# Four source blocks of attention products as one run on TensorE, the last pair of blocks first

## The chip, the cores and the metric

The kernel runs on one core of a Trainium2 chip. A core has several engines that work side by side: TensorE for matrix products (in the profile PE for the products and PEld for the loads of the stationary operand), VectorE (DVE), ScalarE (ACT), GpSimd (POOL) and a queue for transfers (SP). Each engine takes its own list of instructions in a fixed order, and semaphores hold an instruction back until what it reads has been written, or until the buffer that it writes has been read out.

The metric is the time on the device of one execution, in microseconds (us). Before the change it was 3025.95 us, the median of 3 runs (3025.94 to 3026.56). The profile is of one further execution, with a span of 3023.3 us.

## What is computed

Four graph-attention layers run one after the other over 16 graphs of 1024 nodes with 256 features. Each layer normalises the features, cuts them at zero, attends over the graph's neighbours and adds the result to its input. Layer 3, which the change touches, has four heads of 64 features. Cut to what matters:

```
h     = einsum('bnd,hde->bhne', relu(layernorm(x)), W)
weight[i, j] = leaky_relu(e_src[i] + e_dst[j])  where there is an edge
attention    = softmax(weight, over the sources j)
dst   = einsum('bhij,bhje->bhie', attention, h) + bias
out   = layernorm over a head's 64 features (relu(dst) + h) * gamma + beta
x     = x + out
```

The softmax is not normalised ahead of the product. For each head the kernel forms sums of values, each source's features times its unnormalised weight, and beside them totals, the sums of the weights alone, and divides the first by the second at the end.

## The kernel before

**Two streams.** `batch(b)` is a Python generator that writes out the work of one graph and yields estimates of its time. `stream(0)` takes the even graphs and `stream(1)` the odd ones, and the loop at the end of `short_path` (lines 624 to 634) always advances the stream whose estimated clock is behind; the second starts 111 us later (`LAG`). While one stream is in layer 3, the other is in layers 0 to 2 of its graph. The order in which the code is written out is a priority, not the order in which it runs. The framework's scheduler builds each engine's list: of the instructions that are ready in its own model of the run, it takes the one that was written out first. Two means bend this order: `tc.keep_in_program_order(x)` puts x behind the instruction of the same engine that was written out just before it, and `tc.high_priority()`, a context, lets what is written inside it go ahead of ready work outside it.

**Layers 0 to 2** (`attend`, lines 393 to 444). `weigh` (lines 306 to 322) first lets TensorE spread a row of factors over all partitions of the PSUM tile `row` (8 transposes, line 314). There is a single `row` buffer for both streams. VectorE then makes 8 weight tiles of 128 x 1024 out of it, one for each block of 128 source nodes (line 318). Products with line 409 follow, 128 x 128 stationary by 257 moving columns: for the first two blocks of target nodes as each weight tile appears, for the other six afterwards. `project` (lines 267 to 302) makes the values for the next layer: transposes on line 290, products on line 297.

**Layer 3** (lines 478 to 615). Here the values are stationary and the weights move, so that 512 target nodes stream through at once. A head's 64 features and its totals do not fill the array. So `in_tiles` gives each product 32 columns of the array, one of four quadrants (`QUAD` is 32), and four products with different quadrants can run together. All of these matmuls stand on line 517. For a pair of source blocks, `add_values` makes 8 matmuls (two blocks, two halves of the targets, two parts of the features) into the PSUM tile `acc`, and `add_totals` makes 4 (two blocks, two halves) into the PSUM tile `total`. The trace shows each float32 matmul as two records, so that a pair's values are 16 records and its totals 8.

For head 0 the values of each pair follow as soon as VectorE has made the pair's two weight tiles; the totals follow after the row for head 1 is begun, four blocks to a chunk. For heads 1 to 3 a chunk of four blocks has totals and values together: 24 matmuls, 48 records. `pinned`, emptied at the start of every chunk, is the list of the chunk's matmuls so far: from the second on, each is kept behind the one before. That settles the order inside a chunk. It does not keep other ready work of TensorE from coming in between.

The weight tiles of a stream live in 8 buffers (`edges`, `bufs=NI`). So the next head's tiles can only be written when the chunks that read the old ones are through. When a head is finished, ScalarE copies `acc` and `total` out (line 579), TensorE turns them (lines 586 and 594), and VectorE, ScalarE and GpSimd divide, add the bias and normalise (lines 483 to 502).

Of the kernel before, what the change touches and what calls it, by code (L numbers as in the profile page):

```python
# [19 lines left out]

# [2 lines left out]

# [34 lines left out]
def short_path(ctx: ExitStack, tc: tile.TileContext, ins: dict, out: bass.AP, bad: bass.AP):  # L60

    nc = tc.nc
# [3 lines left out]
    NI = N // P  # L66
# [6 lines left out]
    QUAD = P // 4  # L73
# [190 lines left out]
    def accumulator(b: int) -> bass.AP:  # L264
        return psum.tile([P, HALF], F32, name=f"acc{b % 2}")
# [58 lines left out]
    def start(behind, b: int):  # L324

        for t in behind:
            if row_taken == [b]:
                return
            yield t

    def inverse(inv: bass.AP, total: bass.AP):

        nc.vector.tensor_scalar_max(inv, total, TINY)  # L333
        nc.vector.reciprocal(inv, inv)  # L334
# [14 lines left out]
    def batch(b: int):  # L349
# [23 lines left out]
        last = {}  # L373
# [109 lines left out]
        def center(h: int):  # L483

            yh = y[:, :, h, :]
            head = ts(h, E)
            nc.gpsimd.tensor_add(yh, yh, bias[:, head].unsqueeze(1).to_broadcast(shape))  # L487
            nc.vector.scalar_tensor_tensor(yh, yh, 0.0, h3[:, :, head], op0=ALU.max, op1=ALU.add)
            mean = small.tile([P, NI], F32, name="mean")
            nc.vector.tensor_reduce(mean, yh, AX.X, ALU.add)  # L490
            nc.vector.tensor_scalar_mul(mean, mean, 1.0 / E)
            nc.vector.tensor_sub(yh, yh, mean.unsqueeze(2).to_broadcast(shape))
            square = wide.tile(shape, F32, name="wide", bufs=1)
            nc.scalar.activation(square, yh, AF.Square)
            var = small.tile([P, NI], F32, name="var")
            nc.vector.tensor_reduce(var, square, AX.X, ALU.add)  # L496
            return yh, head, inverse_root(var, NI, E, L3_EPS)

        def rescale(yh: bass.AP, head, rstd: bass.AP):
            nc.vector.tensor_mul(yh, yh, rstd.unsqueeze(2).to_broadcast(shape))  # L500
            nc.gpsimd.tensor_mul(yh, yh, gamma[:, head].unsqueeze(1).to_broadcast(shape))
            nc.gpsimd.tensor_add(yh, yh, xb[:, :, head])
# [3 lines left out]
        def weigh3(h: int):  # L506
            if h == H:
                return iter(())
            return weigh(
                b, lambda i: ex[:, i, 2 * H + h : 2 * H + h + 1],  # L510
                lambda j: ex[:, j, H + h : H + h + 1], ALU.max, weights,
            )

        def in_tiles(parts, accT: bass.AP, first: bool, last: bool):

            for n, (values, moving) in enumerate(parts):
                made = nc.tensor.matmul(  # L517
                    accT[ts(n, QUAD), :], values, moving, start=first, stop=last
                )

                if pinned:
                    tc.keep_in_program_order(made)
                pinned.append(made)

        def halves_of(h: int, j: int):
            return [weights[h * NI + j][:, ts(g, HALF)] for g in range(NH)]

        def add_values(h: int, j: int):

            for n in (j + 1, j):  # L530
                parts = [
                    (V3[:, n, h, ts(e, QUAD)], moving)
                    for moving in halves_of(h, n)
                    for e in range(2)
                ]
                in_tiles(parts, acc, n == 1, n == NI - 2)

        def add_totals(h: int, j: int):

            parts = [  # L540
                (V3[:, j + n, h, E:].to_broadcast([P, QUAD]), halves_of(h, j + n)[g])
                for g, n in ((0, 1), (0, 0), (1, 1), (1, 0))
            ]
            in_tiles(parts, total, j == 0, j == NI - 2)

        behind = weigh3(0)
        yield from start(behind, b)
        for h in range(H):


            acc = accumulator(b)
            total = accumulator(b)
            if h == 0:
                for j in range(0, NI, 2):
                    next(behind)
                    next(behind)
                    pinned = []
                    add_values(h, j)
                    yield 1.8
                for _ in behind:  # L560
                    pass
            behind = weigh3(h + 1)
            yield from start(behind, b)
            step = 4
            for first in range(0, NI, step):
                pinned = []
                for j in range(first, first + step, 2):
                    add_totals(h, j)
                    if h > 0:
                        add_values(h, j)  # L570
                for _ in range(step):
                    next(behind, None)
                yield 1.8 if h == 0 else 5.4
            for _ in behind:
                pass
            copies = []
            for accT in (acc, total) if h == 0 else (total, acc):
                copies.append(wide.tile([P, HALF], F32, name="sums"))
                nc.scalar.copy(copies[-1], accT)  # L579
                next(testing)  # L580
                next(coming, None)
            sums, totals = copies if h == 0 else copies[::-1]
            yield 0.5
            turned = psum.tile([P, NG, P], F32, name="misc")
            for i in range(NG):
                nc.tensor.transpose(turned[:, i, :], totals[:, ts(i, P)], ident)  # L586
            inv = small.tile([P, NH, NG], F32, name="inv8")
            nc.vector.tensor_reduce(
                inv, turned[:, :, ::QUAD].rearrange("p i (g n) -> p g i n", n=2), AX.X, ALU.add
            )  # L590
            inverse(inv, inv)
            turned = psum.tile([P, NG, NH, E], F32, name="misc")
            for i in range(NG):
                nc.tensor.transpose(  # L594
                    turned[:, i].rearrange("p g e -> p (g e)"), sums[:, ts(i, P)], ident
                )
            nc.vector.tensor_mul(
                y[:, :, h, :].rearrange("p (g i) e -> p g i e", g=NH),
                turned.rearrange("p i g e -> p g i e"),
                inv.unsqueeze(3).to_broadcast([P, NH, NG, E]),  # L600
            )
            yield 0.5
            if h > 0:
                rescale(*normed.pop())
            normed.append(center(h))
            yield 1.0
# [11 lines left out]
    def stream(first: int):  # L618
        for _ in loading[first]:
            yield 2.0  # L620
        for b in range(first, B, 2):
            yield from batch(b)
# [389 lines left out]
```

## Time and profile before

| what | value |
|---|---|
| time, median of 3 | 3025.95 us |
| span of the profiled run | 3023.3 us |
| granted TensorE clock, mean over the span | 0.993 of full |
| VectorE busy | 2112.7 us, 70% |
| ScalarE busy | 1092.1 us, 36% |
| GpSimd busy | 964.5 us, 32% |
| idle time of VectorE before line 318, ended by line 517 | 51.0 us in 30 waits |

The work repeats. In the chain of work that ended last, the run of 32 matmuls of line 409 that starts at 1165.17 us comes again at 1349.19 us, 184.02 us later, and so on through the run. In each such period one stream does its layer 3 while the other does part of its layers 0 to 2; two periods make a graph of one stream. One period is therefore enough to read, and I use the one from 1065 to 1249 us.

A timeline line gives the start, the time from the first start to the last end of a group of equal instructions, the engine, the line of code, the operation, the tiles and the number of instructions; in brackets the idle time of the engine before it, and what ended it. Matmuls overlap, so that the time a group takes up is read from its start to the start of the next line, not from the second column. In the page's groups "busy" is the union of the times of all instructions of a group and "mean ns" the duration of one of them.

### The profile page before, as it was taken

How to read it: one execution, taken by the hardware profiler on the slowest of the kernel's cores; microseconds unless marked ns; L12 is line 12 of the kernel's file. 1: busy time of each engine (PE TensorE's matmuls, PEld its weight loads, DVE VectorE, ACT ScalarE, POOL GpSimd, SP SyncE). 2: the span in 40 equal slices, each digit the busy share in tenths (PEclk: the TensorE clock that was granted, in tenths of full speed). 3: DMA queues.
4: the chain of work that ended last, by engine and by line, in shares of the span. 5: the costliest groups of instructions: out<-in, count | busy, mean ns of one | idle time of the engine just before them, and what ended most of it. 6: DMA issues, size and time to landing. Idle time of an engine off the chain costs nothing.

```text
span 3023.3 us, 44588 instructions
## 1 busy us (share of the span) xinstructions
PE 2905.2 (96%) x16774; PEld 1960.1 (65%) x16774; DVE 2112.7 (70%) x4467; ACT 1092.1 (36%) x3009; POOL 964.5 (32%) x1455
## 2 busy tenths in 40 slices
PE   7999999999999999999999999999999999999985
PEld 5775857658576675756758566585766857667551
DVE  5657687676866758677576875758667686675756
ACT  2333424243343433424334243433434334243331
POOL 2124324142232423324233242432324234242333
PEclk9999999999999999999999999999999999999997
DMA  7204023030321403122040220302204031110101
GB/s 122 37 8 63 29 29 56 8 49 29 36 49 14 71 2 49 36 28 57 5 50 31 29 56 8 50 29 32 53 11 56 19 50 36 15 29 5 19 21 30
DMA packets 120495, 106.11 MB, mean 35 GB/s; under 512 B 73680, under 2 KB 91216, under 8 KB 120272
## 3 DMA queue, kind: packets, MB, share of 16 engines
q0 software_dynamic: 40448, 67.12, 15.2%
q1 hardware_dynamic: 79824, 36.05, 5.9%
q8 instruction: 135, 2.21, 0.3%
q14 instruction: 88, 0.72, 0.1%
HBM read 153.49 MB, written 33.55 MB: 62 GB/s over the span
## 4 chain that ended last, share of the span: by engine, by line
PE 78%; DVE 12%; POOL 4%; ACT 4%; issue 2%; DMA 1%; SPq 0%; ACTq 0%; POOLq 0%; DVEq 0%
PE acc L409 39%; PE acc L517 21%; PE acc L297 11%; DVE weights L318 6%; PE misc L290 3%; PE row L314 2%; POOL rstd L261 2%; POOL y L487 1%; DVE y L500 1%; DVE V L365 1%; DVE var L496 1%; PE misc L594 1%; ACT adj_i L143 1%; ACT square L281 1%; PE misc L586 1%
## 5 line engine op out<-in xcount | busy, mean ns | idle before, releaser
L409 PE MATMUL acc<-V,weights 128*128 128x257 f32 x6144 | 1452.5, 386 | 24.6 <-ACT above L343 12.8
L409 PEld LDWEIGHTS acc<-V,weights 128*128 128x128 f32 x6144 | 1135.1, 190 | 338.3 <-DVE weights L318 92.7
L517 PE MATMUL acc<-weights,V 128*32 128x512 f32 x6144 | 756.4, 598 | 3.6 <-DVE weights L318 3.6
L318 DVE SCALAR_TENSOR_TENSOR weights<-row,ex,mask 128x1024 f32<-128x1024 f32 x512 | 631.2, 1276 | 91.0 <-PE acc L517 51.0
L297 PE MATMUL acc<-W,hT 128*128 128x259 f32 (+1 forms) x2048 | 522.1, 391 | 39.8 <-ACT hT L292 28.2
L297 PEld LDWEIGHTS acc<-W,hT 128*128 128x128 f32 x2048 | 376.5, 190 | 165.2 <-issue 49.5
L318 DVE SCALAR_TENSOR_TENSOR weights<-row,V,mask 128x1024 f32<-128x1024 f32 x384 | 475.4, 1276 | 7.7 <-PE row L314 7.7
L517 PEld LDWEIGHTS acc<-weights,V 128*32 128x32 f32 x6144 | 174.1, 109 | 379.6 <-issue 370.6
L341 ACT ACTIVATE below<-acc,inv 128x256 f32<-128x256 f32 x256 | 121.3, 474 | 681.0 <-DVE inv L334 404.1
L261 POOL TENSOR_TENSOR rstd<-rstd,minus_half 128x2 f32<-128x2 f32 (+1 forms) x320 | 307.7, 962 | 20.3
L281 ACT ACTIVATE square<-x_b,minus_mean 128x256 bf16<-128x256 f32 x512 | 259.2, 506 | 136.4 <-DVE minus_mean L271 131.7
L333 DVE TENSOR_SCALAR inv<-acc 128x1 f32<-128x1 f32 x256 | 39.7, 155 | 302.5 <-PE acc L409 299.0
L389 POOL TENSOR_TENSOR x_b<-x_b,beta 128x256 f32<-128x256 f32 x128 | 93.6, 731 | 491.1 <-ACT square L281 491.1
L579 ACT COPY sums<-acc 128x512 f32<-128x512 f32 x128 | 75.0, 586 | 413.9 <-PE acc L517 413.9
L260 POOL TENSOR_SCALAR rstd<-squared 128x2 f32<-128x2 f32 x256 | 59.5, 233 | 504.4 <-ACT square L281 503.6
L361 ACT ACTIVATE V<-acc,rstd 128x3 f32<-128x3 f32 x384 | 98.5, 262 | 315.2 <-PE acc L297 312.9
L292 ACT ACTIVATE hT<-misc 128x512 f32<-128x512 f32 x256 | 150.5, 594 | 155.4 <-PE misc L290 155.0
L365 DVE TENSOR_SCALAR V<-acc,rstd,V 128x256 f32<-128x256 f32 x256 | 133.1, 539 | 78.0 <-ACT V L361 77.2
L274 DVE TENSOR_SCALAR centered<-x_b,minus_mean 128x256 f32<-128x256 f32 x512 | 180.4, 383 | 4.3
L138 POOL DMA_DIRECT2D adj_i<-in_adj_dram x128 | 75.6, 590 | 331.0 <-ACT adj_i L143 262.2
L344 DVE SCALAR_TENSOR_TENSOR x_b<-below,x_b 128x256 f32<-128x256 f32 x256 | 117.7, 460 | 87.6 <-ACT below L341 87.4
L290 PE MATMUL misc<-ident,centered 128*128 128x128 f32 x1024 | 159.7, 278 | 15.7 <-DVE centered L274 13.8
(76 smaller groups left out, 2224.8 us busy)
## 6 DMA issues: line engine op xcount, KB each, us to landing
adj_i<-in_adj_dram POOLq DMA_DIRECT2D x128, 256.0 KB, 3.9
x_b<-in_x_dram SPq DMA_DIRECT2D x16, 1024.0 KB, 6.4
narrow<-in_adj_dram POOLq DMA_DIRECT2D x64, 256.0 KB, 9.5
out_dram<-y POOLq DMA_DIRECT2D x32, 512.0 KB, 7.5
mask<-narrow SPq DMA_TRANSPOSE x64, 4.3
W<-in_L_gnn_W_dram SPq DMA_DIRECT2D x3, 256.0 KB, 6.9
weights<-in_L_gnn_a_dram SPq DMA_DIRECT2D x3, 256.0 KB, 9.0
W<-in_L_gnn_W_dram SPq DMA_DIRECT2D x2, 128.0 KB, 7.9
```

Source lines behind the costliest of these rows:

```text
L261: nc.gpsimd.tensor_tensor(r, r, minus_half.to_broadcast([P, n]), op=ALU.pow)
L274: nc.vector.tensor_scalar(centered[:, n, :], xb[:, 2 * pair + n, :], minus_mean[:, n : n + 1], 0.0, op0=ALU.add, op1=ALU.max,)
L281: nc.scalar.activation(square, xb[:, 2 * pair + n, :], AF.Square, bias=minus_mean[:, n : n + 1], accum_out=squared[:, n : n + 1],)
L290: nc.tensor.transpose(turned[:, k, ts(n, P)], centered[:, n, ts(k, P)], ident)
L292: nc.scalar.mul(hT, turned, ROOT_D)
L297: nc.tensor.matmul(projected, hT[:, k, ts(n, P)], W[l][:, k, :], start=(k == 0), stop=(k == NK - 1),)
L318: nc.vector.scalar_tensor_tensor(w, r, c(j), masks[b][:, j // 2, :, j % 2], op0=op, op1=ALU.mult)
L341: nc.scalar.activation(below, acc[:, :D], AF.Exp, scale=inv)
L344: nc.vector.scalar_tensor_tensor(xi, below, 1.0, xi, op0=ALU.min, op1=ALU.add)
L365: nc.vector.tensor_scalar(V[:, i, :D], projected[:, :D], rstd, V[:, i, D : D + 1], op0=ALU.mult, op1=ALU.mult,)
L409: nc.tensor.matmul(accs[i], weights[j][:, ts(i, P)], V[:, j, : D + 1], start=(j == 0), stop=(j == NI - 1),)
L517: made = nc.tensor.matmul(accT[ts(n, QUAD), :], values, moving, start=first, stop=last)
```

## The change

The change lets TensorE run the layer-3 products of four source blocks as one run that nothing interrupts. Three edits work together:

- every matmul of a chunk but the first is written out under `tc.high_priority()`, so that once a chunk has begun, its rest goes ahead of other ready work;
- the two pairs of a chunk are taken in turned order (`first + 2`, then `first`), so that the chunk's first matmul waits for its last-made weight tile, and the others find theirs made; the flags that open and close an accumulation move with the order (blocks 3 and 4 in place of 1 and 6, pairs 2 and 4 in place of 0 and 6);
- head 0's values, in chunks of two blocks until now, come in chunks of four. The estimate yielded for a chunk doubles with it, from 1.8 to 3.6.

The operations and their number stay the same; only their order moves.

```diff
-                made = nc.tensor.matmul(
-                    accT[ts(n, QUAD), :], values, moving, start=first, stop=last
-                )
-
+
+                with tc.high_priority() if pinned else nullcontext():
+                    made = nc.tensor.matmul(
+                        accT[ts(n, QUAD), :], values, moving, start=first, stop=last
+                    )
                 if pinned:
                     tc.keep_in_program_order(made)
                 pinned.append(made)
...
-                in_tiles(parts, acc, n == 1, n == NI - 2)
+                in_tiles(parts, acc, n == 3, n == NI - 4)
...
-            in_tiles(parts, total, j == 0, j == NI - 2)
+            in_tiles(parts, total, j == 2, j == NI - 4)
...
             if h == 0:
-                for j in range(0, NI, 2):
-                    next(behind)
-                    next(behind)
+                for first in range(0, NI, 4):
+                    for _ in range(4):
+                        next(behind)
                     pinned = []
-                    add_values(h, j)
-                    yield 1.8
+                    for j in (first + 2, first):
+                        add_values(h, j)
+                    yield 3.6
                 for _ in behind:
                     pass
             behind = weigh3(h + 1)
             yield from start(behind, b)
-            step = 4
-            for first in range(0, NI, step):
+
+            for first in range(0, NI, 4):
                 pinned = []
-                for j in range(first, first + step, 2):
+                for j in (first + 2, first):
                     add_totals(h, j)
                     if h > 0:
                         add_values(h, j)
-                for _ in range(step):
+                for _ in range(4):
                     next(behind, None)
                 yield 1.8 if h == 0 else 5.4
```

More of the change, by code (lines that the diff above doesn't have):

```diff
@@ L23 @@
-from contextlib import ExitStack
+from contextlib import ExitStack, nullcontext
 from itertools import chain, islice
```

## The prediction

> **What bounds the kernel.** I read the page first: the engines' busy times, the chain that ended last, the costliest groups.
>
> ```profile
> PE 2905.2 (96%) x16774; PEld 1960.1 (65%) x16774; DVE 2112.7 (70%) x4467; ACT 1092.1 (36%) x3009; POOL 964.5 (32%) x1455
> PE 78%; DVE 12%; POOL 4%; ACT 4%; issue 2%; DMA 1%; SPq 0%; ACTq 0%; POOLq 0%; DVEq 0%
> L517 PE MATMUL acc<-weights,V 128*32 128x512 f32 x6144 | 756.4, 598 | 3.6 <-DVE weights L318 3.6
> L318 DVE SCALAR_TENSOR_TENSOR weights<-row,ex,mask 128x1024 f32<-128x1024 f32 x512 | 631.2, 1276 | 91.0 <-PE acc L517 51.0 <-PE row L314 40.0
> ```
>
> TensorE is busy 96% of the span and is 78% of the chain; VectorE is the 12% beside it. Line 517 waits for weights for 3.6 us in the whole run, so no stall is to be removed. But a busy TensorE isn't one at its peak, and the share says nothing of single stretches. So I read one period (1065 to 1249 us), by stretch and then by the timeline. Columns of the stretches: length, then busy time and instructions of PE, PEld, DVE, ACT, POOL.
>
> ```profile
> 1147.00:1165.00 18.00, 17.55 (x107) 8.09 (x105) 14.35 (x21) 4.58 (x9) 5.96 (x8) 1.00 0.15 16
> 1182.00:1218.00 36.00, 36.00 (x242) 20.95 (x241) 24.25 (x48) 16.23 (x38) 15.90 (x18) 1.00 0.34 53
> ```
>
> In both TensorE looks full. The timeline shows that they are not alike:
>
> ```profile
> 1142.04 4.48 PE L517 MATMUL acc<-weights,V 128*32 128x512 f32 x34
> 1146.45 1.09 PE L314 MATMUL row<-ident,V 128*128 128x128 f32 x8
> ...
> 1150.38 1.07 PE L517 MATMUL acc<-weights,V 128*32 128x512 f32 x8
> 1151.38 1.13 PE L409 MATMUL acc<-V,weights 128*128 128x257 f32 x4
> 1152.44 1.07 PE L517 MATMUL acc<-weights,V 128*32 128x512 f32 x8
> ...
> 1161.55 1.06 PE L517 MATMUL acc<-weights,V 128*32 128x512 f32 x6
> 1162.54 1.13 PE L409 MATMUL acc<-V,weights 128*128 128x257 f32 x4
> 1163.51 1.04 PE L314 MATMUL row<-ident,ex 128*128 128x128 f32 x8
> 1165.17 7.20 PE L409 MATMUL acc<-V,weights 128*128 128x257 f32 x32 [0.63 <-ACT above L343]
> 1172.31 2.76 PE L517 MATMUL acc<-weights,V 128*32 128x512 f32 x18
> ```
> ```profile
> 1136.04 9.62 DVE L318 SCALAR_TENSOR_TENSOR weights<-row,ex,mask 128x1024 f32<-128x1024 f32 x8 [2.88 <-PE acc L517]
> 1160.61 1.27 DVE L318 SCALAR_TENSOR_TENSOR weights<-row,V,mask 128x1024 f32<-128x1024 f32 x1
> ```
> ```profile
> 1199.24 5.36 PE L517 MATMUL acc<-weights,V 128*32 128x512 f32 x48
> ```
>
> From 1136.04 to 1161.88 (1160.61 + 1.27) VectorE makes sixteen weight tiles with other work between; its only idle stretches there are 0.48, 0.19 and 1.25 us. TensorE follows at that pace, four matmuls of line 409 per tile with pieces of line 517 as filling. **This stretch belongs to VectorE.** From 1165 to 1218 us TensorE has work without a gap but for 0.6 us at its start: **that stretch belongs to TensorE.**
>
> **The Trainium skill.** "TensorEngine Tiling (Array Packing)", Key Properties: "Changing tiling mode (not just tile) drains the TensorE". Line 517 has tiles of 128 x 32, all else of 128 x 128; the trace agrees that a change costs, 0.33 us for one there and back (worked out below). "TensorE: Matmul & The Clock Gate", Part 3: matmuls on different tiles of the array run together. It agrees: a record lasts 598 ns, yet 48 take up 5.29 us (1199.24 to the next line at 1204.53), 110 ns each. The same page, Part 2, has matmuls keep their program order, only weight loads are pulled ahead; so a matmul that waits for a weight tile holds back whatever stands behind it on TensorE. Nothing in this trace contradicts that, but it has no long such wait to show it.
>
> **Part 1, unbroken chunks.** In the timeline I count the pieces into which line 517 falls in the period: 6 for head 0, 8 for head 1, 5 for head 2, 2 for head 3, together 21 (323 in the run, so some 15 periods). Unbroken it would be 4 + 2 + 2 + 2 = 10. Price of a break: 48 records take 5.29 us and 8 take 1.00 (1150.38 to 1151.38), so a further record takes 4.29/40 = 0.107. For line 409, 32 take 7.14 (1165.17 to 1172.31) and 4 take 1.06: 6.08/28 = 0.217. Eight and four in a long run would take 0.86 + 0.87 = 1.73; as separate pieces they take 2.06. **One break costs 0.33 us**, eleven cost 3.6.
>
> There is a second loss. The piece of 34 takes 4.41 us where 32 would take 1.00 + 24 x 0.107 = 3.57: its last matmul (2 records) stands alone in the array, and takes 0.84 us, as long as four quadrants together. The piece of 18 is the same: 2.69 us, where 16 take 1.85 (1123.28 to 1125.13). Their counterparts of 14 and 6 records take as long as 16 and 8. That is 0.84 us in head 1 and again in head 2.
>
> Gross gain per period: head 0, 2 breaks, 0.67; head 1, 6 breaks and a torn group, 2.0 + 0.84 = 2.84; head 2, 3 breaks and a torn group, 1.0 + 0.84 = 1.84; head 3 nothing. Sum 5.35 us.
>
> **What of it counts.** Head 2's pieces (from 1172.31) lie in TensorE's stretch: its 1.84 counts in full. Its eight weight tiles are made by 1177.17, when the unbroken first chunk would be ending (1172.31 + 5.29 = 1177.60), so no new wait appears. Head 1's 2.84 lies in VectorE's stretch, where TensorE can only wait longer for tiles; nothing else is ready to fill it, since the other stream's next products need all eight tiles. What counts is the end: the last tile is ready at 1161.88, its products start at 1162.54, behind a piece of line 517 that would no longer be there. That is 0.66 us. Head 0's 0.67 is judged with the waits.
>
> **Part 2, the waits added.** Head 0's values now start at the fourth and eighth tile instead of every second. The eighth is made at 1130.42. Before, the last values end at 1133.90; now 16 matmuls follow it, 3.57 us, so they end at 1134.1. Behind them on TensorE stand the row for head 1 (1.02) and the first chunk of totals (1.85), whose end frees the buffers for head 1's tiles. VectorE's wait at 1136.04 (2.88 us, ended by line 517) ends 1.12 us into that chunk: after the totals of its first pair. With the pairs turned, tiles 2 and 3 come free there and tiles 0 and 1 at the end, 0.86 us (8 x 0.107) later. The trace doesn't show which buffer VectorE's next tile takes. If any free one, its start moves by the 0.2 of the values; if the oldest, by 0.2 + 0.86 = 1.06. In the first case the other stream's row (1146.45) loses instead: head 1's chunk from 1142.04 would end at 1147.3, so the row comes 0.88 later. **I take 1.0 us later for VectorE's stretch in either case**, with 0.2 and 2 as ends. While TensorE waits for the fourth and eighth tile it can do line 409 and 297 work that it had anyway, and 0.7 us that nothing fills is part of this delay. The later release in head 2 (VectorE waits 0.53 us at 1189.04 for line 517) costs nothing: head 3's chunks come at 1199 and 1208, long after.
>
> **Part 3, priority and estimates.** No instruction is added; yields in head 0 sum to what they were. Pushed back are transposes and projections of the other stream, by at most one chunk (5.29 us); from 1165 on TensorE does them later in the same full stretch, at no cost.
>
> **Sum.** Per period 1.84 + 0.66 - 1.0 = 1.5 us gained. Times 15: 22.5 us. 3026 - 23 = **3003 us**.
>
> **Rivals.**
>
> - *All of the gross gain counts.* 5.35 x 15 = 80 us: 2946. For it: TensorE is 78% of the chain, and the two streams might settle so that VectorE's stretch shrinks. Against it: VectorE's 0.48, 0.19 and 1.25 us of idle time in its 26 us. A half-way case lies at 2975.
> - *Slower: a row has to wait for an unbroken chunk.* There is one `row` buffer; the transposes of line 314 fall into a chunk twice in the period (1146.45 and 1178.60), and VectorE starts on tiles only after them. If a row in VectorE's stretch comes half a chunk (2.6 us) later, beyond what I counted, the period loses 2.6 - 1.5 = 1.1 us: 3042. For it: 47.7 us of VectorE's waits before line 318 are for rows already. Against it: at 1178.60 the chunk would be over by then.
> - *No change.* Head 2's gain is eaten by a delay at the upper end: 1.84 + 0.66 - 2 = 0.5 us, or 3018; with little more, 3026.
>
> **Chances.** The forecast, from 2985 to 3018, 0.45; more of the gross gain, 2940 to 2985, 0.2; no change 0.1; slower 0.25. Below 2950 I leave 0.08, above 3046 0.1; so the range is 2950 to 3046. Faster by over 0.2% (below 3020) has 0.65, within 0.2% 0.10, slower 0.25.
>
> **What would show it.** Right: ten pieces of line 517 per period, of 32, 16 and 48 records; TensorE's busy time lower by up to 80 us, and a good part of that back as idle time before line 409 ended by line 318, in the stretch where VectorE makes sixteen tiles; VectorE's wait for line 517 at head 1 longer by up to 1 us; the period near 182.5 us. Wrong: VectorE's wait for rows growing by over 2 us a period (slower), VectorE's stretch getting shorter (faster), or pieces that stay broken.

## The result and the profile after

The changed kernel takes 2989.39 us, the median of 4 runs (2988.22 to 2990.52), against 3025.94 us before (4 runs). The ratio is 0.9881, with a 95% interval of 0.9866 to 0.9896: 36.5 us or 1.2% faster. The forecast was 3003 us.

These lines of the page of the changed kernel answer to those shown of the kernel before. Line 517 has become line 519.

```profile
PE 2839.7 (95%) x16774; PEld 1986.1 (66%) x16774; DVE 2148.9 (72%) x4467; ACT 1090.0 (36%) x3009; POOL 956.7 (32%) x1455
PE 55%; DVE 28%; issue 8%; POOL 5%; ACT 3%; DMA 1%; POOLq 0%; SPq 0%; ACTq 0%; DVEq 0%
L519 PE MATMUL acc<-weights,V 128*32 128x512 f32 x6144 | 692.1, 597 | 11.4 <-DVE weights L318 7.5
L318 DVE SCALAR_TENSOR_TENSOR weights<-row,ex,mask 128x1024 f32<-128x1024 f32 x512 | 630.3, 1273 | 102.5 <-PE row L314 95.7
```

TensorE is busy 65.5 us less, nearly all of it on the layer-3 products (756.4 to 692.1 us for the same 6144 records). The span fell by 34.4 us, so about half came back as idle time of TensorE (118 us before, 149 after). VectorE has more of the chain, 28% after 12%, and its wait ahead of the tiles is no longer for line 517 but for rows.

The timeline of TensorE in the changed kernel, in the stretch that answers to 1142 to 1172 us of before:

```profile
1131.98 5.36 PE L519 MATMUL acc<-weights,V 128*32 128x512 f32 x48
1137.27 1.09 PE L314 MATMUL row<-ident,V 128*128 128x128 f32 x8
1138.29 5.36 PE L519 MATMUL acc<-weights,V 128*32 128x512 f32 x48
1143.57 4.60 PE L409 MATMUL acc<-V,weights 128*128 128x257 f32 x20
1148.78 3.52 PE L409 MATMUL acc<-V,weights 128*128 128x257 f32 x12 [0.60 <-DVE weights L318]
1152.13 1.04 PE L314 MATMUL row<-ident,ex 128*128 128x128 f32 x8
1153.24 7.20 PE L409 MATMUL acc<-V,weights 128*128 128x257 f32 x32
```

Head 1's two chunks stand whole. In the whole run line 519 has 142 pieces, where 323 were before. The periods are so regular that kernels can be laid over each other. I measure from the start of the row for head 0 (line 314, at 1119.27 us before and 1109.84 after) to five later events, all read from timelines. "Behind the projection" means behind the matmuls of line 297 that follow head 2's first chunk:

| us after head 0's row | before | after | gained |
|---|---|---|---|
| first tile of head 1 (VectorE) | 16.77 | 17.14 | -0.37 |
| start of the last of the sixteen tiles | 41.34 | 39.99 | 1.35 |
| run of 32 products of line 409 (1165.17; 1153.24) | 45.90 | 43.40 | 2.50 |
| 16 products behind the projection (1183.38; 1171.49) | 64.11 | 61.65 | 2.46 |
| next period | 184.02 | 181.36 | 2.66 |

So nearly the whole gain is there by the end of head 1, in the stretch that I had given to VectorE. Across head 2, between the third and fourth row, nothing is gained. That is the reverse of the forecast.

Why is VectorE's stretch shorter? In the kernel before it holds an idle time of 1.25 us; VectorE first, then ScalarE, of the kernel before:

```profile
1160.01 0.69 DVE L496 TENSOR_REDUCE var<-wide 128x8 f32<-128x512 f32 x1 [1.25 <-ACT wide L494]
```
```profile
1157.73 0.59 ACT L579 COPY sums<-acc 128x512 f32<-128x512 f32 x1 [16.20 <-PE acc L517]
1158.22 1.15 ACT L143 ACTIVATE adj_i<-adj_i,minus_half 128x1024 bf16<-128x1024 bf16 x1
...
1159.36 0.62 ACT L494 ACTIVATE wide<-y 128x512 f32<-128x512 f32 x1
1162.67 0.59 ACT L579 COPY sums<-acc 128x512 f32<-128x512 f32 x1 [2.69 <-PE acc L517]
1163.15 1.15 ACT L143 ACTIVATE adj_i<-adj_i,minus_half 128x1024 bf16<-128x1024 bf16 x1
...
1164.65 0.47 ACT L343 ACTIVATE above<-acc,inv 128x256 f32<-128x256 f32 x1
```

And ScalarE of the changed kernel at the same work:

```profile
1145.24 0.19 ACT L143 ACTIVATION_READ_ACCUMULATOR adj_i<-adj_i,minus_half 128x1 f32 x1
1145.77 0.63 ACT L494 ACTIVATE wide<-y 128x512 f32<-128x512 f32 x1 [0.34 <-DVE y L492]
```

Before, head 0's square (line 494) stood in ScalarE's list behind the first of the two copies of head 1's results (line 579). That copy waited for line 517, whose pieces were spread out to 1162.5 us. VectorE's `var` (line 496) waited for the square, and the last tile stood behind `var`. The broken pieces thus held VectorE up by way of ScalarE. After the change the copies are done early (1142.05 and 1143.71 us), and the square waits only for its own input.

From the first tile of head 1 to the last of the sixteen the stretch is 1.72 us shorter (24.57 before, 22.85 after). The 1.25 us are most of it. The rest is an idle time of 0.48 us before the other stream's first tile, which waited for its row (1147.57 us before); now the first product of y stands ahead of that tile in VectorE's list and fills the time.

The table has a further 1.15 us between the last tile and the run of 32. Before, the products of the last tile started 0.66 us after it was ready, behind a piece of line 517; after the change 0.06. And the run of 32 waited 0.63 us for line 343, which stood on ScalarE behind the second copy, and so again behind line 517. From the row ahead of it to the run took 1.66 us before and takes 1.11 now.

### The profile page after: what moved, and what is told of

Read it like the earlier page. It is cut to its first block, busy times and chain, and to the rows that moved or that the text cites. A ratio compares the mean times of both kernels' runs of the same rounds, so it can differ in the third digit from the quotient of the medians.

```text
span 2988.9 us, 44636 instructions
## 1 busy us (share of the span) xinstructions
PE 2839.7 (95%) x16774; PEld 1986.1 (66%) x16774; DVE 2148.9 (72%) x4467; ACT 1090.0 (36%) x3009; POOL 956.7 (32%) x1455
## 4 chain that ended last, share of the span: by engine, by line
PE 55%; DVE 28%; issue 8%; POOL 5%; ACT 3%; DMA 1%; POOLq 0%; SPq 0%; ACTq 0%; DVEq 0%
PE acc L409 33%; DVE weights L318 19%; PE acc L297 9%; PE acc L519 9%; PE misc L290 2%; POOL rstd L261 2%; POOL y L487 1%; ACT square L281 1%; DVE x_b L345 1%; DVE V L365 1%; PE row L314 1%; DVE x_b L344 1%; ACT below L341 1%; DVE y L488 1%; DVE var L496 1%
## 5 line engine op out<-in xcount | busy, mean ns | idle before, releaser
L409 PE MATMUL acc<-V,weights 128*128 128x257 f32 x6144 | 1436.6, 385 | 26.2 <-DVE weights L318 15.7
L519 PE MATMUL acc<-weights,V 128*32 128x512 f32 x6144 | 692.1, 597 | 11.4 <-DVE weights L318 7.5
L519 PEld LDWEIGHTS acc<-weights,V 128*32 128x32 f32 x6144 | 189.4, 110 | 422.9 <-issue 415.3
L344 DVE SCALAR_TENSOR_TENSOR x_b<-below,x_b 128x256 f32<-128x256 f32 x256 | 136.8, 534 | 82.7 <-ACT below L341 82.5
L274 DVE TENSOR_SCALAR centered<-x_b,minus_mean 128x256 f32<-128x256 f32 x512 | 168.5, 357 | 5.2
L290 PEld LDWEIGHTS misc<-ident,centered 128*128 128x128 f32 x1024 | 121.3, 141 | 60.1 <-issue 26.9
```

Source lines behind the costliest of these rows:

```text
L274: nc.vector.tensor_scalar(centered[:, n, :], xb[:, 2 * pair + n, :], minus_mean[:, n : n + 1], 0.0, op0=ALU.add, op1=ALU.max,)
L290: nc.tensor.transpose(turned[:, k, ts(n, P)], centered[:, n, ts(k, P)], ident)
L344: nc.vector.scalar_tensor_tensor(xi, below, 1.0, xi, op0=ALU.min, op1=ALU.add)
L409: nc.tensor.matmul(accs[i], weights[j][:, ts(i, P)], V[:, j, : D + 1], start=(j == 0), stop=(j == NI - 1),)
L519: made = nc.tensor.matmul(accT[ts(n, QUAD), :], values, moving, start=first, stop=last)
```

## The experiments

**Which of the three edits does it, and whose stretch is it?** I had formed theory V from the table: the gain is VectorE's, and comes from the order of its list, in which the first product of y now stands ahead of the other stream's first tile. Theory T: each avoided break is worth the same.

The priority alone, on the kernel before:

```diff
-                made = nc.tensor.matmul(
...
+                with tc.high_priority() if pinned else nullcontext():
+                    made = nc.tensor.matmul(
...
```

> The kernel before with the priority context alone: pairs in their old order, head 0 in chunks of two. TensorE's list then has 184 pieces of layer-3 products (323 before, 142 after the change), and VectorE's list in the sixteen-tile stretch has the first product of y ahead of the other stream's first tile, as after the change. Theory V (the gain came from VectorE's stretch, shorter by 1.35 us net a period, and from the end of that stretch, 1.15 us): nearly the whole gain, 2985 to 2995 us. Theory T (each avoided break is worth the same, 36.5 us for 181 breaks): 139 breaks, 28 us, 2998 us.

Measured 2990.47 us, ratio 0.9887 (0.9872 to 0.9902): the whole change. Its list has 184 pieces and head 0 in pieces of two blocks. The run of 32 starts at 43.40 as in the changed kernel, although its first tile of head 1 starts at 16.76, not 17.14. Turned pairs and chunks of four bring nothing beside the priority. The time lies in V's range and 8 us below T's figure, which speaks for V; the next runs speak against both.

The other two edits without the priority:

```diff
-                with tc.high_priority() if pinned else nullcontext():
+                with nullcontext():
```

> The changed kernel without the priority context: turned pairs and head 0 in chunks of four stay. TensorE's list has 291 pieces, VectorE's has the other stream's first tile ahead of y as in the kernel before. Both theories: little, 3015 to 3026 us (T: 32 breaks, 6 us). If the turned order by itself carries the change, it is near 2990.

Measured 3043.03 us, ratio 1.0064 (1.0050 to 1.0077): slower, which neither theory expected. Up to the 16 products behind the projection this kernel is nearly as the one before (64.28 against 64.11 us); most of the loss comes after, where a matmul is torn off a chunk, as in the next experiment.

The order of VectorE's list alone, on the kernel before (the edges of order are shortened here and below):

```diff
+    for b in range(B - 1):        # the other stream's first tile of layer 1
+        later, sooner = tiles_of[b + 1], y_of[b]    # behind y's first product
+        tc.add_manual_dep(later.ins, sooner.ins.name, NoSync, ...)
```

> The kernel before with one edge of order on VectorE: the other stream's first tile of layer 1 comes behind the first product of y of head 0. TensorE's pieces stay broken (306 of them). Theory V: VectorE's stretch gets shorter by 1.3 to 1.7 us a period, 15 periods, 20 to 26 us: 3000 to 3006 us. Theory T: 17 breaks at 0.2 us, 3 us: 3022 us.

Measured 3041.61 us, ratio 1.0059 (1.0045 to 1.0073). Both theories fall, V by 35 us or more and T by 20. The timeline, VectorE then TensorE (head 0's row is at 1123.64 us; line 409 is here 412, line 517 is 520):

```profile
1160.88 3.67 DVE L319 SCALAR_TENSOR_TENSOR weights<-row,V,mask 128x1024 f32<-128x1024 f32 x3
```
```profile
1163.51 1.91 PE L520 MATMUL acc<-weights,V 128*32 128x512 f32 x10
1165.34 2.87 PE L412 MATMUL acc<-V,weights 128*128 128x257 f32 x12
1168.04 1.04 PE L315 MATMUL row<-ident,ex 128*128 128x128 f32 x8
1169.15 7.20 PE L412 MATMUL acc<-V,weights 128*128 128x257 f32 x32
...
1202.88 1.05 PE L520 MATMUL acc<-weights,V 128*32 128x512 f32 x2
1203.85 1.14 PE L297 MATMUL acc<-W,hT 128*128 128x259 f32 x4
1204.93 5.35 PE L520 MATMUL acc<-weights,V 128*32 128x512 f32 x46
```

VectorE's last tile starts at 39.62 us, 1.72 earlier than before. Both of its idle times are gone, although the pieces stay broken: with y earlier, the square ran on ScalarE at 1159.21 us, ahead of the copies (1161.77 and 1165.45). So the way by ScalarE is closed here, while TensorE's pieces are still broken. But the run of 32 starts at 45.51, only 0.39 earlier: the last tile is ready at 1164.5 us (1160.88 + 3.67), and TensorE, slowed by its pieces, is busy with the products of the last tiles (line 412) until 1168.0. In this stretch **both engines were close to their limit**: shortening VectorE's work alone leaves TensorE's broken pieces.

Two losses follow. From the run of 32 to the 16 products it takes 18.96 us, against 18.21 before; in head 2's pieces, still broken, TensorE now waits 0.64 us for VectorE's line 274. The other is the last lines above: a lone matmul (2 records) ahead of the chunk. From the 16 products behind the projection to those behind head 3's first chunk it takes 22.09 us, against 21.14 before; 22.09 also in the two other kernels with this piece (turned order alone, and head 1 alone below). A torn matmul with its break costs 0.95 us here.

The reverse edge on the changed kernel:

```diff
+        later, sooner = y_of[b], tiles_of[b + 1]
```

> The changed kernel with the reverse edge: the first product of y of head 0 comes behind the other stream's first tile of layer 1, as in the kernel before. TensorE's pieces stay unbroken (142). Theory V: the stretch is as long as before again, 20 to 26 us are lost: 3009 to 3015 us. Theory T: the pieces are what counts, 2989 us.

Measured 2973.38 us, ratio 0.9831 (0.9817 to 0.9844): 16 us faster than the changed kernel, where V expected a loss and T no difference. The last tile starts at 40.27 and the run of 32 at 43.67, 0.27 us later than with the change. So the order of y on VectorE is worth 0.27 us; unbroken pieces keep the stretch short with either order. The further gain comes in head 2: in most periods the 16 products behind the projection start at 60.41, not 61.65. The next experiment tells why.

No run moves the square alone ahead of the copies in ScalarE's list. That the way by ScalarE held VectorE up is read from the waits. Both kernels above that close it agree: the stretch of the sixteen tiles is 1.44 us shorter in this one and 1.71 in the one with y first.

**Where did head 2's gain go?** TensorE in the changed kernel behind head 2's first chunk, then ScalarE:

```profile
1167.15 0.73 PE L314 MATMUL row<-ident,ex 128*128 128x128 f32 x5 [0.40 <-DVE inv L333]
1168.84 0.66 PE L596 MATMUL misc<-ident,sums 128*128 128x128 f32 x4 [0.96 <-ACT hT L292]
1169.34 0.49 PE L314 MATMUL row<-ident,ex 128*128 128x128 f32 x3
```
```profile
1167.83 0.47 ACT L341 ACTIVATE below<-acc,inv 128x256 f32<-128x256 f32 x1 [3.13 <-DVE inv L334]
1168.20 0.59 ACT L292 ACTIVATE hT<-misc 128x512 f32<-128x512 f32 x1
```

The copy hT could run when its transposes (line 290, 1165.66 to 1166.32) are through. It stands behind line 341, which waits for VectorE, and starts only at 1168.20, 1.88 us later. The transposes of y (line 596) wait for the `misc` buffer that hT empties, and the last three of the row for head 3 wait behind them. Before, hT ran at 1175.69, ahead of line 341. Theory S: this gives head 2's gain back. The edge that tests it:

```diff
+    for b in range(B):      # line 341 of layer 1's third block behind hT of the first pair
+        tc.add_manual_dep(below_of[b].ins, hT_of[b].ins.name, NoSync, ...)
```

> The changed kernel with one edge of order on ScalarE: the exponential of layer 1's third block (line 341 of the listing) comes behind the copy hT of the first pair (line 292). Theory S (head 2's 1.84 us were saved on TensorE but given back because hT stood behind line 341, which waits 3.13 us for VectorE; transposes of y and the row for head 3 waited behind it on TensorE, 0.40 and 0.96 us idle): 1.0 to 1.3 us a period come back, 2970 to 2975 us. Rival (TensorE would wait for VectorE's tiles there anyway): unchanged, 2989 us.

Measured 2970.73 us, ratio 0.9818 (0.9805 to 0.9831). With this edge (line 596 is 602, 292 stays, 341 is 344; head 0's row is at 1103.76 us):

```profile
1160.28 0.60 ACT L292 ACTIVATE hT<-misc 128x512 f32<-128x512 f32 x1 [1.66 <-PE misc L290]
1160.77 0.47 ACT L344 ACTIVATE below<-acc,inv 128x256 f32<-128x256 f32 x1
```
```profile
1160.93 0.66 PE L602 MATMUL misc<-ident,sums 128*128 128x128 f32 x4
```

Line 602 waits no more. In most periods the 16 products come at 60.13 (60.42 in the one shown) and the period is 179.81 us. From the run of 32 to the 16 products it then takes 16.73 us, against 18.25 with the change and 18.21 before. Theory S is shown. This is the lowest time of all versions, 1.8% below the kernel before; the next one and the kernel with the reverse edge lie within 0.2% of it.

The kernel with the reverse edge agrees without an edge on ScalarE. There line 341 still stands ahead of hT, but its factor from VectorE is ready at 1158.97 us, before hT's transposes are through (1159.07); hT starts at 1159.44, and the run of 32 and the 16 products are 16.74 us apart.

The same edge on the priority alone:

> Priority alone on the kernel before, with the same edge of order on ScalarE. If turned pairs and chunks of four in head 0 bring nothing and theory S holds: as the changed kernel with that edge, 2970 to 2977 us. If S is wrong, 2990 us.

Measured 2972.45 us, ratio 0.9820 (0.9807 to 0.9834), with the 16 products at 60.13 again: S holds there too, and the other two edits stay without effect.

**Heads one by one.** The priority for head 1 or head 2 alone, on the kernel before:

```diff
+                with tc.high_priority() if pinned and h in (1,) else nullcontext():
```

> The kernel before with the priority context for head 1 alone; 246 pieces on TensorE, with a matmul torn off a later chunk in most periods (pieces of 1 and 23 matmuls), which costs 0.84 + 0.33 us by the trace of before. Theory U (head 1's pieces count in full, 2.84 us, since they also delay ScalarE's copies and through these VectorE): 2.84 - 1.17 = 1.7 us a period, 25 us, about 3000 us. The prediction's own step (0.66 us of head 1 counts): 0.66 - 1.17, 8 us slower, 3032 us.

Measured 3014.23 us, ratio 0.9962 (0.9948 to 0.9976), between the two expectations. At the run of 32 it has gained 2.50 us (43.40), all that the changed kernel has: theory U, which counted 2.84, is near on head 1. Then 1.05 us are lost in head 2, whose pieces are still broken and where TensorE now waits 0.93 us for VectorE's line 274 (the expectation left that out), and 0.95 on the torn matmul. The period is 183.51 us.

> The kernel before with the priority context for head 2 alone; 277 pieces on TensorE. The prediction's step (head 2's 1.84 us count in full, they lie in TensorE's stretch): 28 us, 2997 us. Theory S (given back in the wait for hT): 3020 to 3026 us.

Measured 3008.51 us, ratio 0.9941 (0.9928 to 0.9955), again between the two. Nothing is gained at the run of 32 (45.90); 1.49 us are gained at the 16 products (62.62), and the period is 182.53 us. Here hT runs at 1174.81, right behind its transposes and ahead of line 341. Head 2's gain is real by itself; it is lost only where line 341 waits for VectorE ahead of hT.

## Why the prediction was right or wrong

The direction was right and the time lies in the range of the forecast, near its faster end; what carried it was in large part not what I said.

- **Price of a break and of a torn matmul: right in kind, a fifth too high.** Their sum was to be 5.35 us a period. The records of line 519 take 64.3 us less busy time, 4.3 for each of the 15 periods that I counted. The torn matmul with its break, 0.84 + 0.33 by my sum, was measured at 0.95 us. Head 2, 1.84 by my sum, gave 1.49 alone. Why all three are lower by a fifth I did not work out.
- **"Head 1's 2.84 lies in VectorE's stretch, where TensorE can only wait longer": wrong, and the largest error.** I counted 0.66 us; head 1 alone gave 2.50. The 0.66 itself came about as 0.60. Beside it stand 1.35 us by which VectorE's last tile comes earlier and 0.55 ahead of the run of 32. I had seen VectorE's idle times of 0.48 and 1.25 us, and the 0.63 on TensorE, and not asked what stood behind them. The 1.25 and the 0.63 led by way of ScalarE's copies to line 517 itself, and TensorE was as late as VectorE at the end, as the kernel with y first showed. The rival "the two streams might settle so that VectorE's stretch shrinks" was true of this head.
- **"Head 2's 1.84 counts in full": wrong for the change.** It gave -0.04 us there (2.46 - 2.50), 1.49 when changed alone, and 1.48 with the edge on ScalarE (18.21 - 16.73). I looked for waits for weight tiles and found none; the wait was for hT, in another engine's list.
- **The waits added, 1.0 us: too high.** Head 1's first tile started 0.37 us later and this cost nothing: with it and without (priority alone) the run of 32 starts at 43.40. I had assumed that the row would stay ahead of the totals; the scheduler ran head 0's second chunk and its first totals as one piece of 48, ahead of the row (nine pieces a period, not ten), so that VectorE waits 4.28 us for the row there and not for line 519.
- **15 periods: too many.** There are 13 between regular starts; the first and last graphs stand partly alone.
- **"No change" and "slower by waiting rows"** did not come about. VectorE's wait for rows did grow, from 47.7 to 96.3 us in all, while its wait for line 517 fell from 51.0 to 6.8: one took the place of the other. By my own list this growth, 3.2 us for each of 15 periods, was a sign of a slower kernel; it was none. The shorter stretch of VectorE, my sign of a faster one, did come.

By the forecast's terms: -1.0 became about 0, 0.66 became 2.50, 1.84 became -0.04; the sum 1.5 became 2.66 with 0.2 from later in the period, which I did not trace. That the terms of heads 1 and 2 add up to 2.50 in the forecast and to 2.46 in the run is luck: the first was far too low and the second far too high. So the forecast landed in its range, but not for its reasons.

## What to carry to other kernels

When an idle time of about a microsecond stands in a stretch that you give to one engine, follow it to what ended it, and then to what stood ahead of that in its engine's list; it may lead back to the work that you are about to change. A gain on one engine can be lost where another engine's list has, ahead of what is needed next, an instruction that waits for a third: here TensorE's gain in head 2, by line 341 ahead of hT. After such a change look for the first idle time behind the faster part; one edge of order there was worth about half as much again as the change (18.7 us beside 36.5).

## What was not expected of the hardware

In these traces a single matmul on a 128 x 32 tile, with no neighbour on the other three, holds TensorE as long as four side by side. A piece of 2 records takes 0.97 us (1202.88 to 1203.85, with y first) and one of 8 takes 1.00 (1150.38 to 1151.38 before). In three kernels one such matmul torn off a chunk cost 0.95 us a period with its break, more than the break alone at 0.33 by the forecast's sum. That one matmul is most of the 1.12 us a period by which turned pairs and chunks of four without the priority made the kernel slower.
